# Scaled bias copies behind the relus, the flag's sum an iteration later, new steps and scatter times of the last blocks, and second buffers, in a fused graph network kernel

## The chip, the cores and the metric

The kernel runs on one core of one Trainium2 chip. The metric is the device time of one execution in microseconds (us), lower is better. A ratio is the mean time of one kernel's fast runs over the mean of the other's fast runs of the same rounds, so it is not quite the ratio of the medians that stand beside it.

The span of a profiled execution is about 1.7 us shorter than its time (613.8 us and 615.49 us for the kernel before). Spans and points in time below are those of the trace.

In the profile's lines PE is TensorE, PEld its weight loads, DVE is VectorE, ACT ScalarE and POOL GpSimd; L567 is line 567 of that run's file, so numbers differ by a few between kernels. Of the tiles, z, hps, hT, mu and ma are in PSUM (TensorE's results), y and h are the relus of the two layers, sh the deviations of layer 0, ys the scatter sum of the messages, and uh, uy and uo the stages of a block's update.

## The reference, cut to what matters

There are 128 graphs of 64 nodes with 128 features, and an adjacency matrix for each.

```python
def _layernorm(x, g, b):
    mu = jnp.mean(x, axis=-1, keepdims=True)
    var = jnp.mean(jnp.square(x - mu), axis=-1, keepdims=True)
    return (x - mu) * jax.lax.rsqrt(var + EPS) * g + b

def _mlp(x, w0, b0, g0, be0, w1, b1, g1, be1, w2, b2):
    h = jax.nn.relu(x @ w0 + b0)
    h = _layernorm(h, g0, be0)
    h = jax.nn.relu(h @ w1 + b1)
    h = _layernorm(h, g1, be1)
    return h @ w2 + b2
# ... (f_i, f_j: the features of both ends of each pair of nodes)
pair_feats = jnp.concatenate([f_i, f_j], axis=-1)
messages = _mlp(pair_feats, msg_w0, ...) * coupling_matrix[..., None]
agg = jnp.sum(messages, axis=2)
upd_in = jnp.concatenate([part_feats, agg], axis=-1)
updated = part_feats + _mlp(upd_in, upd_w0, ...)
```

## The kernel before

The kernel packs the existing edges into chunks of 512 slots and runs the message MLP on these chunks only: 160 chunks (NCHK), in 32 groups of five (QC). The 128 graphs form 16 blocks of ten chunks, each with one update MLP. Everything is placed by hand: `at(n, place, f)` puts a step into iteration n, and each iteration runs its places in a fixed order. Each engine's instructions then stand in the order in which they were issued.

```python
L1 = QC + 3                  # layer 1 of chunk n-8 runs in iteration n
for n in range(last + 1):
    run(n, "a")
    run(n, "m")
    if 0 <= n - L1 < NCHK:
        layer1(n - L1)       # z (TensorE), y = relu(z) (ScalarE)
    run(n, "b")
    if n < NCHK:
        layer0(n)            # hps (TensorE), h = relu (ScalarE)
    if 0 <= n - 1 < NCHK:
        stats0(n - 1)        # transposes hT (TensorE), bn_stats (VectorE)
    run(n, "k")
    if 0 <= n - L1 < NCHK:
        stats1(n - L1)
    for k in ("x", "x1", "x2", "e0", "e1", "e"):
        run(n, k)
```

The tile z has one PSUM bank, and so have hT and mu. In the last chunks, layer 1 takes turns between the banks of z and hps. The steps of a block's update are placed by a tuple t of offsets. STEADY serves blocks 0 to 12, and LAST serves the last three blocks. The last block is done in two halves.

```python
STEADY = (1, 2, 3, 3, 4, 7, 8, 6, 8, 9, 12, 13, 11, 14, 15)
# ...
at(n + t[4], "m", layer_out, u, "uh", "m0")    # uh = relu(mu + m0), statistics
at(n + t[7], "a", upd_root0, u)                # um_sd, the standard deviation
at(n + t[7], "a", upd_shift, u)                # usdb
at(n + t[8], "x", lambda u: layer(u, ("uhT", W["u1c"])), u)
at(n + t[9], "m", layer_out, u, "uy", "usdb")  # uy = relu(mu + usdb)
# ...
at(n + t[13], "x", lambda u: layer(u, ("uyT", W["u2c"])), u)
at(n + t[14], "m", finish, u)                  # uo (VectorE), output DMA

def upd_shift(u):
    u.usdb = wide("usdb", u)
    for q in range(u.n):
        nc.scalar.activation(u.usdb[:, q, :], W["bu1b"], AF.Copy, scale=u.sd[:, q:q + 1])
```

A flag at the end tells whether any graph had too many edges for the packed path. Its sum is a small matmul into the one mu bank, and VectorE reads it from there.

```python
at(NCHK - 3, "x", flag_sum)      # FL["b"] = ubank(), one matmul
at(NCHK - 1, "m", flag_out)      # read by VectorE
```

## Time and profile before

| what | value |
|---|---|
| time, median of three runs | 615.79 us (615.77 to 616.52) |
| span of the profiled execution | 613.8 us |
| TensorE busy | 94% of the span |
| first load for z (start of the steady part) | 35.71 us |
| block 12's last layer, mu from u2c (end of the steady part) | 556.27 us |
| end of the last uo | 609.81 us |
| period of a block | 35.11 us |

The table cuts the span in four: the start up to 35.71 us, a steady part of 520.56 us, a tail of 53.54 us and some 4 us of closing output.

The view of busy time by stretches gives, for each stretch, its length, then the busy time of PE, PEld, DVE, ACT and POOL with the number of instructions, then the granted TensorE clock (PEclk, 1.00 is full), the share of the DMA engines and GB/s. In the tail of the kernel before:

```profile
560.00:562.00 2.00, 2.00 (x12) 2.00 (x10) 0.00 (x0) 0.56 (x1) 0.00 (x0) 0.52 0.81 213
562.00:564.00 2.00, 2.00 (x15) 1.83 (x15) 0.72 (x4) 0.82 (x3) 0.00 (x0) 0.62 0.36 82
```

TensorE is fully busy here and runs at half clock for most of it: 2.00 x (1 - 0.52) + 2.00 x (1 - 0.62) = 1.7 us of full-speed work are lost. This stretch follows the wait of 2.1 us for uo. The end of the tail, behind a third long wait of 2.2 us (for uy of block 15, ending at 603.23), is at half clock too:

```profile
606.00:608.00 2.00, 1.49 (x7) 1.19 (x7) 0.60 (x4) 1.02 (x4) 0.14 (x1) 0.50 0.01 4
```

### The profile page before, as it was taken

Reading aid. Unit: us, or ns where it says so; the run is one execution under the profiler, and the core shown is the slowest. Engines: PE = TensorE matmul, PEld = TensorE weight load, DVE = VectorE, ACT = ScalarE, POOL = GpSimd, SP = SyncE. Lnnn points to the kernel's source line nnn. Section 1 sums busy time; section 2 is a strip of 40 time slices with the busy share of each in tenths; the row PEclk is TensorE's granted clock in tenths of the full one; section 3 lists DMA queues with packets and bytes.
Section 4 is the critical chain, followed back from the end, with each engine's and each line's share of the span. In section 5 each row is a group of like instructions: output and inputs, shape, how many; then the busy total and the mean of one; then the engine's idle time right before and its main releaser. Section 6 shows DMA issues by size and latency. Waiting matters only on the chain.

```text
span 613.8 us, 15572 instructions
## 1 busy us (share of the span) xinstructions
PE 579.7 (94%) x5393; PEld 535.0 (87%) x5393; DVE 480.0 (78%) x1947; ACT 397.4 (65%) x845; POOL 296.3 (48%) x837
## 2 busy tenths in 40 slices
PE   5898999999999999999999999999999999998884
PEld 4686889898989999998999989898999999898783
DVE  5657688897979788797978879797978878784685
ACT  5666566776766567766766677676656776653433
POOL 1532455554636565453646555463656545343442
PEclk9989999999999999999999999999999999998996
DMA  4654535544455545644544554345453443531101
GB/s 109 145 126 116 105 88 134 98 123 91 109 140 99 130 90 132 115 99 120 117 122 102 131 102 124 88 112 139 109 134 77 119 116 92 104 87 40 33 9 38
DMA packets 91087, 63.86 MB, mean 104 GB/s; under 512 B 57462, under 2 KB 74876, under 8 KB 91004
## 3 DMA queue, kind: packets, MB, share of 16 engines
q1 hardware_dynamic: 90716, 62.69, 44.5%
q8 instruction: 44, 0.72, 0.5%
q14 instruction: 39, 0.32, 0.2%
q10 hardware_dynamic: 288, 0.13, 0.1%
HBM read 6.82 MB, written 4.19 MB: 18 GB/s over the span
## 4 chain that ended last, share of the span: by engine, by line
PE 82%; ACT 7%; DVE 6%; issue 1%; POOL 1%; DMA 1%; SPq 0%; DVEq 0%; ACTq 0%; POOLq 0%
PE z L566 20%; PE hps L516 12%; PE ys L645 11%; PE hT L525 10%; PE mu L704 8%; PE z L563 7%; PE mu L437 4%; PE ma L690 3%; PE mk L490 3%; ACT usdb L726 2%; ACT y L569 2%; PE ma L423 1%; DVE st L576 1%; ACT abh L446 1%; DVE st L529 1%
## 5 line engine op out<-in xcount | busy, mean ns | idle before, releaser
L529 DVE BATCH_NORM_STATS2 st<-hT 128x6 f32<-128x128 f32 x640 | 142.0, 284 | 67.0 <-PE hT L525 66.1
L566 PEld LDWEIGHTS z<-w1c,h 128*128 128x128 f32 x1248 | 164.6, 192 | 6.6
L566 PE MATMUL z<-w1c,h 128*128 128x128 f32 x1248 | 165.2, 275 | 0.0
L576 DVE BATCH_NORM_STATS2 st<-y 128x6 f32<-128x128 f32 x640 | 137.2, 276 | 4.0 <-ACT y L569 4.0
L569 ACT ACTIVATE y<-z 128x512 f32<-128x512 f32 x156 | 92.7, 594 | 65.9 <-PE z L566 65.3
L247 POOL TENSOR_TENSOR m_d<-st 128x20 f32<-128x20 f32 x62 | 15.7, 254 | 224.3 <-DVE st L529 199.6
L519 ACT ACTIVATE h<-hps,b0c 128x512 f32<-128x512 f32 x160 | 109.2, 682 | 3.3 <-PE hps L516 3.2
L632 POOL TENSOR_TENSOR w<-oh,m_q 128x320 f32<-128x320 f16 x126 | 91.1, 739 | 17.9 <-issue 12.0
L525 PE MATMUL hT<-ident,h 128*128 128x128 f32 x640 | 98.3, 277 | 0.0
L516 PE MATMUL hps<-s,abl 128*128 128x512 f32 (+3 forms) x256 | 92.9, 374 | 0.4 <-ACT h L519 0.4
L525 PEld LDWEIGHTS hT<-ident,h 128*128 128x128 f32 x640 | 77.1, 142 | 9.9 <-DVE st L529 0.3
L563 PE MATMUL z<-b1t,sdT 80*128 80x512 f32 x156 | 76.3, 489 | 6.0 <-ACT y L569 6.0
L516 PE MATMUL hps<-s,abh 128*128 128x512 f32 (+3 forms) x256 | 79.3, 328 | 0.0
L446 ACT CAST abh<-mu 128x512 fp32r<-128x512 f32 x32 | 18.7, 585 | 91.9 <-PE mu L439 91.9
L645 PE MATMUL ys<-y,w 128*64 128x128 f32 x1280 | 77.4, 275 | 0.1
L645 PEld LDWEIGHTS ys<-y,w 128*64 128x64 f32 x1280 | 69.4, 137 | 7.5 <-issue 7.0
L498 DVE TENSOR_TENSOR j<-mk,cmpt 128x320 fp32r<-128x320 f32 x126 | 59.5, 472 | 1.6 <-PE mk L490 1.6
L462 ACT ACTIVATE d<-slot,mid 128x640 f16<-128x640 f16 x64 | 53.3, 833 | 0.0
L516 PEld LDWEIGHTS hps<-s,abl 128*128 128x128 f32 x256 | 50.1, 196 | 1.8 <-ACT i L474 0.9
L516 PEld LDWEIGHTS hps<-s,abh 128*128 128x128 f32 x256 | 50.2, 196 | 0.0
L474 ACT CAST i<-tp 128x640 fp32r<-128x640 f16 x63 | 45.2, 717 | 1.8 <-DVE tp L468 1.8
L453 DVE TENSOR_TENSOR abl<-mu,abh 128x512 fp32r<-128x512 f32 x32 | 22.1, 690 | 27.9 <-ACT abh L446 27.7
(225 smaller groups left out, 991.4 us busy)
## 6 DMA issues: line engine op xcount, KB each, us to landing
s<-i SPq DMA_DIRECT2D x126, 160.0 KB, 2.7
s<-j SPq DMA_DIRECT2D x126, 160.0 KB, 2.6
xn<-in_x_dram SPq DMA_DIRECT2D x15, 256.0 KB, 3.8
out_dram<-uo SPq DMA_DIRECT2D x15, 256.0 KB, 2.4
an<-in_adj_dram SPq DMA_DIRECT2D x16, 128.0 KB, 2.7
oh<-tp SPq DMA_TRANSPOSE x64, 2.7
xn<-in_x_dram SPq DMA_DIRECT2D x2, 128.0 KB
out_dram<-uo SPq DMA_DIRECT2D x2, 128.0 KB
```

The costliest lines, as they stand in the source:

```text
L462: nc.scalar.activation(D[p], slot, AF.Abs, bias=blocks[b]["mid"][:, q:q + 1], scale=-1.0)
L498: nc.vector.tensor_tensor(JR[p][:, c], MK.pop((p, k))[:, 0:HC], cmpt[:, c], op=ALU.is_equal)
L516: nc.tensor.matmul(ps[:, c:c + w], lhsT=ab[:, g % 4, :], rhs=s, start=(k == 0), stop=(k == 1))
L519: nc.scalar.activation(H[n], ps, AF.Relu, bias=b0c)
L525: nc.tensor.transpose(ps[:, t, :], H[n][:, t * P:(t + 1) * P], ident)
L529: nc.vector.bn_stats(ST0[q][:, CH * c + t, :], ps[:, t, :])
L563: nc.tensor.matmul(ps, lhsT=SD[q], rhs=W["b1t"][:, CH * c:CH * c + CH, :], start=True, stop=False, skip_group_check=True)
L566: nc.tensor.matmul(ps[:, t, :], lhsT=h[:, t * P:(t + 1) * P], rhs=W["w1c"], start=False, stop=True, skip_group_check=True)
L569: nc.scalar.activation(Y[n], ps, AF.Relu)
L576: nc.vector.bn_stats(ST1[q][:, CH * c + t, :], Y[n][:, t, :])
L632: (nc.vector if p == NP - 2 else nc.gpsimd).tensor_tensor(WT[p][:, :, g, :], OH[p][:, :, g * N:(g + 1) * N], Q[q][:, k:k + TG].unsqueeze(2 ...
L645: nc.tensor.matmul(YS[b][g * N:(g + 1) * N, k, :], lhsT=w[:, t, g, :], rhs=y, start=(t == 0), stop=(t == TG - 1))
```

## The change

The intent: take the scaled bias copies (usdb) out of the way of the relu y that frees the z bank; shorten the tail by reordering the steps of the last blocks, the scatter weights and the flag; and allow more overlap with second buffers. The core of the diff:

```diff
         def centred(w, g, name):
-            wg = const.tile([P, C], F32, name=name + "_g")
             def product():
+                wg = W[name, "g"] = const.tile([P, C], F32, name="wg", bufs=2)
 # ... (beb likewise, shared in two buffers)
-                                        bufs=2 if name in ("uo", "xo") else 1)
+                                        bufs=2 if name in ("uo", "xo", "m0") else 1)
 # ... steps of blocks 13, 14 and the two halves of 15
-        LAST = ((1, 2, 3, 3, 4, 5, 6, 6, 6, 7, 8, 9, 9, 9, 10),
-                (0, 4, 5, 5, 6, 7, 8, 8, 8, 9, 10, 11, 11, 11, 12),
-                (1, 1, 2, 2, 3, 3, 4, 5, 4, 6, 6, 7, 7, 7, 8),
+        LAST = ((1, 2, 3, 3, 4, 5, 6, 6, 8, 9, 10, 11, 11, 11, 12),
+                (0, 5, 6, 6, 7, 7, 8, 8, 8, 9, 9, 10, 10, 10, 11),
+                (2, 2, 3, 3, 4, 4, 5, 5, 5, 6, 6, 7, 7, 7, 8),
                 (1, 1, 2, 2, 3, 3, 4, 4, 4, 5, 5, 6, 6, 6, 7))
-                    units = [units[0][:3] + (2, 0)]
+                    units = [units[0][:3] + (-5, -4)]
-                units = [(Unit(b, 2, 2, nc.vector, zbank), NCHK + L1 + 1, LAST[3], 1, -3),
-                         (Unit(b, 0, 2, nc.gpsimd, hbank), NCHK + L1, LAST[2], 2, -2)]
+                units = [(Unit(b, 2, 2, nc.vector, zbank), NCHK + L1 + 1, LAST[3], 1, 1),
+                         (Unit(b, 0, 2, nc.gpsimd, hbank), NCHK + L1 - 1, LAST[2], 3, 3)]
-                at(n + t[7], "a", upd_shift, u)
+                at(n + t[7], "x", upd_shift, u)
 # ... (scatter weights, reduce, root_of, turn_root, root_out, root1_of of the
 #      last groups: an iteration earlier or later)
-        at(NCHK - 3, "x", flag_sum)
-        at(NCHK - 1, "m", flag_out)
+        at(NCHK - 2, "x", flag_sum)
+        at(NCHK, "m", flag_out)
 # ...
+            if n == NCHK:
+                stats0(n - 1)
             if 0 <= n - L1 < NCHK:
                 layer1(n - L1)
 # ...
-            if 0 <= n - 1 < NCHK:
+            if 0 <= n - 1 < NCHK - 1:
                 stats0(n - 1)
```

More of the change, by code (lines that the diff above doesn't have):

```diff
@@ L184, in empty @@
                 W[name] = const.tile([P, C], F32, name=name)
-                nc.vector.tensor_tensor(W[name], wg, ps[:, :C], op=ALU.subtract)
+                nc.vector.tensor_tensor(W[name], W.pop((name, "g")), ps[:, :C], op=ALU.subtract)
             return product, empty
@@ L199, in shift @@
         def shift(w, be, bias, name):
-            beb = const.tile([P, P], F32, name=name + "_b")
             def fn(ps):
+                beb = const.tile([P, P], F32, name="beb", bufs=2)
                 nc.scalar.copy(beb, be.to_broadcast([P, P]))
@@ L829, in edge_path @@
             for g in range(2):
-                late = h if q == NQ - 3 else (2 * h + g + 1) // 2
-                at(*((NCHK + L1, "b") if last else (q * QC + QC + L1 + 2 + late, "e1")), weights, p, g)
-            at(NCHK + L1 + 1 if last else q * QC + SC - (q == NQ - 3), "x1", reduce, p)
+                wait = h + 2 if q == NQ - 3 else h + 1 if q == NQ - 2 else 2 + (2 * h + g + 1) // 2
+                at(*((NCHK + L1, "b") if last else (q * QC + QC + L1 + wait, "e1")), weights, p, g)
+            at(NCHK + L1 + 1 if last else q * QC + SC - (q >= NQ - 3), "x1", reduce, p)
         for q in range(NQ):
@@ L837, in edge_path @@
             at(*((n, "e1") if last else (n + 1, "b")), root_of, q)
-            at(n + 1, "b" if last else "x", turn_root, q)
-            at(*((n + 1, "x") if last else (n + 2, "a")), root_out, q)
+            at(*((n + 2, "b") if last else (n + 1, "x")), turn_root, q)
+            at(n + 2, "x" if last else "a", root_out, q)
             at(n + L1 - last, "e1", var1_step, q)
-            at(n + L1 + (0 if last else 2), "a", root1_of, q)
-            at(n + L1 + (0 if last else 2), "m", inverse_of, q)
+            wait = 0 if last else 1 if q == NQ - 2 else 2
+            at(n + L1 + wait, "a", root1_of, q)
+            at(n + L1 + wait, "m", inverse_of, q)
         warm = ubank()
```

## The prediction

> **What bounds the kernel now.** I read the page first: engine shares, then the chain that ended last.
>
> ```profile
> span 613.8 us, 15572 instructions
> PE 579.7 (94%) x5393; PEld 535.0 (87%) x5393; DVE 480.0 (78%) x1947; ACT 397.4 (65%) x845; POOL 296.3 (48%) x837
> PE 82%; ACT 7%; DVE 6%; issue 1%; POOL 1%; DMA 1%; SPq 0%; DVEq 0%; ACTq 0%; POOLq 0%
> ```
>
> TensorE is the bound: 82% of the chain lies on it. The busy table by stretches gives PE 49.1 to 49.6 of every 50 us between 100 and 500 us, but 17.7 of 22 in 558 to 580 and 6.0 of 14 in the last stretch. So a saving counts in two places only: waits of PE inside the steady part, and the tail after about 557 us. Next I asked whom PE's weight loads waited for.
>
> ```profile
> PEld z L563 <- ACT y L569: 9.4, 14, 0.7
> ...
> PEld ma L549 <- DVE sh L544: 3.1, 1, 3.1
> ...
> PEld mu L929 <- DVE uo L740: 2.1, 1, 2.1
> ```
>
> The first is steady: once per block, every 35.1 us. There is a single PSUM bank for z, so a chunk's layer-1 matmul needs the relu (y, ACT) of the chunk before to have read it. The other two are single waits of the tail. One such block, ScalarE's timeline (start, duration, engine, line, operation):
>
> ```profile
> 353.43 0.58 ACT L446 CAST abh<-mu 128x512 fp32r<-128x512 f32 x1 [3.12 <-PE mu L439]
> 353.91 0.30 ACT L257 ACTIVATE um_sd<-um,eps_c 128x4 f32<-128x4 f32 x1
> 354.25 1.28 ACT L726 ACTIVATE usdb<-bu1b,um_sd 128x128 f32<-128x128 f32 x4
> 355.43 0.57 ACT L569 ACTIVATE y<-z 128x512 f32<-128x512 f32 x1
> 355.91 0.67 ACT L519 ACTIVATE h<-hps,b0c 128x512 f32<-128x512 f32 x1
> 356.48 0.72 ACT L474 CAST i<-tp 128x640 fp32r<-128x640 f16 x1
> 357.09 0.83 ACT L462 ACTIVATE d<-slot,mid 128x640 f16<-128x640 f16 x1
> 357.82 0.30 ACT L271 ACTIVATE m_sq<-m_v,eps_c 128x20 f32<-128x20 f32 x1
> 358.02 0.58 ACT L569 ACTIVATE y<-z 128x512 f32<-128x512 f32 x1
> ```
>
> and PE's weight loads beside it:
>
> ```profile
> 356.06 0.19 PEld L563 LDWEIGHTS z<-b1t,sdT 80*128 80x128 f32 x1 [0.69 <-ACT y L569]
> ...
> 358.66 0.19 PEld L563 LDWEIGHTS z<-b1t,sdT 80*128 80x128 f32 x1
> ```
>
> The four scaled bias copies (usdb) stand ahead of y, so y starts 0.7 us late and PE waits 0.69. But see what follows: from 353.91 ScalarE has no gap until the next y ends at 358.60, and PE comes to the next z at 358.66 with no idle time noted. That second z is on the edge already. The trace holds a control: the first block has no update yet, hence no usdb.
>
> ```profile
> 75.88 0.60 ACT L569 ACTIVATE y<-z 128x512 f32<-128x512 f32 x1 [0.73 <-PE z L566]
> ...
> 78.49 0.59 ACT L569 ACTIVATE y<-z 128x512 f32<-128x512 f32 x1
> ```
>
> ```profile
> 79.14 0.19 PEld L563 LDWEIGHTS z<-b1t,sdT 80*128 80x128 f32 x1 [0.49 <-ACT y L569]
> ```
>
> There y waits only for its matmul, and PE stalls at the second z instead.
>
> **What the Trainium skill says.** (1) "TensorE: Matmul & The Clock Gate", section "Architectural detail": the ACT and DVE queues are strictly first in, first out. The trace agrees: y at 355.43 stood behind usdb though z was computed at 354.70. (2) "ScalarE: Activation LUTs", section "What ACT_TABLE_LOAD costs": 186 ns + 0.833 ns per column, about 93 ns for a pointer operand, and neighbours overlap by about 93 ns. For 128 columns that is 386 ns; the trace has a median of 387, and 1.18 us from usdb's start to y's. (3) The first page, section "Part 1: The HAM clock gate": the array falls to half clock after an idle window of about 3.4 us. The stretches agree on the half: after the 2.1 us wait for uo the granted clock reads 0.52 in 560 to 562 and 0.62 in 562 to 564. Yet the 3.1 us wait for sh at 572 to 575 was followed by 1.00, so which stall trips it I can't foretell. (4) "SBUF — State Buffer", section "SBUF: two separate sides": VectorE and GpSimd lock a shared port. The last variance steps on VectorE (m_v, m_s, m_d) took 0.74 us beside GpSimd's multiplies, and 0.18 without: it agrees.
>
> **The change part by part.**
>
> *Bias copies behind the relus (13 steady blocks, usdb at 108 to 530 us).* The order listing shows sd, y, h, usdb, i, d, m_sq, y instead of sd, usdb, y, h, i, d, m_sq, y; nothing is removed. Now y starts when z is ready: by the control 1.31 us after abh (74.57 to 75.88), so at 353.43 + 1.31 = 354.74. It ends near 355.33, and PE, free at 355.37, no longer waits: 0.69 won. But usdb now lies between the two y's. From y to y the control takes 78.49 - 75.88 = 2.61 us; with usdb's 1.18 that is 3.79. The second y starts at 354.74 + 3.79 = 358.53 and ends at 359.11, so PE's second z loads at 359.17, where it loaded at 358.66. PE reaches it at 358.66 - 0.69 = 357.97 and stalls 1.2 us. ScalarE now idles half a microsecond before the first y, and that lands on the path, so each block loses 359.17 - 358.66 = **0.51 us**. PE has no slack later in the block to win it back. 13 x 0.51 = **+6.6 us**.
>
> *Flag's sum an iteration later.* It used the one mu bank right after block 12's last layer and had to wait for uo. Now z of the next iteration goes first. PE is free at 557.27 rather than 559.44. The flag still waits for uo, which now stands behind block 14's bias (m0, 4 operations, 1.12 us, moved ahead of it): uo ends at 560.3, PE arrives at 559.85, so a stall of 0.5 is left. The 40-matmul ys load starts at 560.5 instead of 563.8: -3.3 us, of which about 1.8 is the half clock that I expect not to be tripped here.
>
> *stats0 of the last chunk before layer 1; steps of blocks 13 to 15; scatter times.* The transposes hT of chunks 158 and 159 now stand together, with one bank, so the second waits for VectorE's statistics: about 1.0 us lost (565.1 to 566.1). In return the last layer-0 deviation (sh) comes at 571.1, not 574.9, and hps, u1c and z fill the wait: of 3.1 us about 0.35 is left. Walking on through queues in their listed order, with rows' durations: ys at 571.2; hps, uy, z, u2c, hps, z, hps until 580.5; the second last ys at 580.5 (before: 588.8, but then with the ysum layer ahead of it). VectorE's last variance runs from 582.3 to 583.4 with GpSimd idle (before 587.5 to 590.3, slowed by the port). Its weights are ready at 585.9, the mu layer (1.75 us) ends at 586.3, and the last ys runs 586.4 to 588.8, where it ended at 595.0: -6.2 us in all. After it, the before kernel needs 14.8 us to its last uo (609.8). By the same walk the new order needs 13.4 (block 15's halves no longer go back to front, and its bias is computed early): last uo at 602.2. Tail: 609.8 - 602.2 = **-7.6 us**. The closing 4.0 us of output DMA stay.
>
> *Second m0 buffer, wg and beb shared in two buffers.* Capacity only; each is written again only iterations (2 us and more each) after its last reader: 0.
>
> Sum: 615.8 - 7.6 + 6.6 = **614.8 us**.
>
> **Rivals.** (a) *The steady stall simply goes.* Then 13 x 0.69 = 9.0 us are saved and, with the tail, the time is 615.8 - 9.0 - 7.6 = 599 us, faster by 2.7%. For it: the noted wait does vanish. Against it: ScalarE's gapless run to 358.60 and the control's stall of 0.49. It would need i or d to run elsewhere. (b) *The tail yields little*: the new transpose stall, a half-clock window tripped by it (about 1.7 us each), or the copy chain of block 15's halves on ScalarE takes the saving. With a tail of only -3, 615.8 + 6.6 - 3 = 619.4. For it: every tail wait stands on another engine's queue, and my walk assumes no new surprise. (c) *The steady loss is smaller*, if h or the DMA-fed casts already pad the run: with 0.2 a block, 615.8 + 2.6 - 7.6 = 610.8. I see no padding in the rows.
>
> **Range and chances.** The steady term rests on two measured blocks; I give it +5.5 to +7.5. The tail is a walk of some 45 us by hand; -5 to -9. Taken together, 80% is 611.8 to 617.6. Two per cent is 12.3 us, so faster means under 603.5, which needs rival (a): 5%. Slower means over 628.1, for which both terms must go wrong: 1%.
>
> **What would show it.** Steady: the wait of z on y is still there once a block, now near 1.2 us in place of 0.69, at the second z; the period grows from 35.11 to about 35.6 us. If the period shrinks to 34.4, rival (a) holds and my reading of ScalarE's queue is wrong. Tail: a wait of about 0.5 us for uo at the flag; no half-clock window near 560; a new wait of about 1 us of hT on VectorE; sh's wait below 0.5; from the flag's uo to the last uo about 42 us (before 50.5). If half clock appears inside the tail, rival (b).

## More of the kernel before

The timed executions quoted here were all in the fast state. The one exception is a single execution of one experiment, whose state is unknown, and that is said there.

## The result, and the profile after

The changed kernel took 613.11 us (median of four runs, 611.84 to 613.53) against 615.93 us of the kernel before in the same rounds (four runs, 615.77 to 616.52). The ratio is 0.9949, with a 95% interval of 0.9932 to 0.9966: the same within 2%, and 0.5% shorter.

The head of the page of the changed kernel:

```profile
span 611.1 us, 15571 instructions
PE 574.7 (94%) x5393; PEld 530.1 (87%) x5393; DVE 479.3 (78%) x1947; ACT 397.2 (65%) x845; POOL 294.8 (48%) x837
```

The span fell by 2.7 us, the work is the same, and TensorE is still the bound. The chain of work that ended last can't be used here: in this trace it stops after a single step on VectorE. So I cut both spans in four, as above, by the starts of the same instructions:

| | start | steady part | tail | closing output | span |
|---|---|---|---|---|---|
| before | 35.71 | 520.56 | 53.54 | 4.0 | 613.8 |
| after | 33.56 | 527.32 | 46.36 | 3.9 | 611.1 |
| difference | -2.15 | +6.76 | -7.18 | -0.1 | -2.7 |

The change does two opposite things of about equal size. Whom the weight loads of the changed kernel waited for (total us, times, longest us):

```profile
PEld z L561 <- ACT y L567: 15.1, 14, 1.1
...
PEld hT L523 <- ACT h L517: 1.3, 1, 1.3
...
PEld ma L547 <- DVE sh L542: 0.7, 1, 0.7
PEld mu L928 <- DVE uo L738: 0.6, 1, 0.6
```

The steady wait for y, 9.4 us before, has grown to 15.1 us. The two long waits of the tail (3.1 for sh and 2.1 for uo) have shrunk to 0.7 and 0.6, the third (2.2 for uy) to 0.4, and a new one of 1.3 has come at hT. The view names h for that one, but this h had ended at 570.03, 0.7 us before the load at 570.77. The matmul's own line in TensorE's timeline names VectorE's statistics (st), which ended at 570.65:

```profile
570.80 0.63 PE L523 MATMUL hT<-ident,h 128*128 128x128 f32 x4 [1.08 <-DVE st L527]
```

ScalarE's timeline in one block, the same place as in the prediction (start, duration, engine, line, operation, and in brackets the idle time before it and what ended that):

```profile
354.93 0.59 ACT L444 CAST abh<-mu 128x512 fp32r<-128x512 f32 x1 [3.13 <-PE mu L437]
...
356.24 0.60 ACT L567 ACTIVATE y<-z 128x512 f32<-128x512 f32 x1 [0.53 <-PE z L564]
...
357.30 1.27 ACT L724 ACTIVATE usdb<-bu1b,um_sd 128x128 f32<-128x128 f32 x4
...
360.02 0.58 ACT L567 ACTIVATE y<-z 128x512 f32<-128x512 f32 x1
```

and the weight loads of TensorE that follow those two y:

```profile
356.89 0.19 PEld L561 LDWEIGHTS z<-b1t,sdT 80*128 80x128 f32 x1
...
360.65 0.19 PEld L561 LDWEIGHTS z<-b1t,sdT 80*128 80x128 f32 x1 [1.13 <-ACT y L567]
```

The first y now starts as soon as z is there, with ScalarE idle for 0.53 us before it, and its z no longer waits. But usdb lies between the two y, which are 360.02 - 356.24 = 3.78 us apart, and the second z waits 1.13 us. From abh to that second load it was 358.66 - 353.43 = 5.23 us before and is 360.65 - 354.93 = 5.72 us now: 0.49 us more in this block. From block to block the first kernel's period is 35.11 us and the second's 35.63 us.

In the tail, the stretch by busy time in which the flag's wait for uo ends (at 564.98):

```profile
564.00:566.00 2.00, 1.61 (x24) 1.34 (x24) 2.00 (x10) 1.21 (x3) 1.50 (x4) 1.00 0.05 14
```

The clock stays at 1.00, here and in every stretch of the tail in which TensorE still works.

### The profile page after: what moved, and what is told of

Its sections match the earlier page's. It is cut to its first block, busy times and chain, and to the rows that moved or that the text cites. A ratio compares the mean times of both kernels' runs of the same rounds, so it can differ in the third digit from the quotient of the medians.

```text
span 611.1 us, 15571 instructions
## 1 busy us (share of the span) xinstructions
PE 574.7 (94%) x5393; PEld 530.1 (87%) x5393; DVE 479.3 (78%) x1947; ACT 397.2 (65%) x845; POOL 294.8 (48%) x837
## 5 line engine op out<-in xcount | busy, mean ns | idle before, releaser
L245 POOL TENSOR_TENSOR m_d<-st 128x20 f32<-128x20 f32 x62 | 17.1, 276 | 229.7 <-DVE st L527 206.3
L561 PEld LDWEIGHTS z<-b1t,sdT 80*128 80x128 f32 x156 | 29.4, 189 | 21.9 <-ACT y L567 15.1
```

The costliest lines, as they stand in the source:

```text
L561: nc.tensor.matmul(ps, lhsT=SD[q], rhs=W["b1t"][:, CH * c:CH * c + CH, :], start=True, stop=False, skip_group_check=True)
```

## The experiments

The theory after the result: (1) the steady loss is all due to where usdb stands in ScalarE's queue, (2) the tail's gain is due to the flag and the new steps together, (3) the buffers do nothing, (4) the start is chance. Eleven runs were made, three of them repetitions, all with correct results. This is the cut of their profiled executions:

| kernel | start | steady part | tail | span |
|---|---|---|---|---|
| before | 35.71 | 520.56 | 53.54 | 613.8 |
| after | 33.56 | 527.32 | 46.36 | 611.1 |
| copies_only | 32.56 | 527.09 | 55.42 | 619.5 |
| copies_back | 34.23 | 520.58 | 46.90 | 605.6 |
| copies_early | 32.80 | 512.24 | 46.33 | 595.3 |
| buffers_only | 32.74 | 520.76 | 53.60 | 611.5 |
| early_stats_back | 34.33 | 512.26 | 46.07 | 596.7 |
| early_again | 34.28 | 512.14 | 46.36 | 596.7 |
| flag_only | 34.26 | 520.59 | 51.55 | 610.2 |
| copies_twice | 35.81 | 550.34 | 46.34 | 636.4 |
| steps_only | 33.16 | 520.74 | 50.82 | 608.6 |
| after_again | 34.21 | 527.31 | 46.34 | 611.8 |
| buffers_again | 33.23 | 520.62 | 55.50 | 613.6 |

Steady part and tail move independently to within about half a microsecond, so their effects can be added.

### The copies alone, undone, and moved to an idle place

**copies_only**: the kernel before, with one line of the change.

```diff
-                at(n + t[7], "a", upd_shift, u)
+                at(n + t[7], "x", upd_shift, u)
```

> The kernel before with one edit: the four scaled bias copies are issued after the two relus of the same iteration. My theory (they now lie between the two relus y of which the second frees the z bank): 13 blocks x 0.52 us, so about 622.6 us, wait of z on y 1.13 us a block, period 35.63 us. Rival (the copies were simply in the way): 13 x 0.69 us less, 606.9 us, period 34.4 us. The start can differ by about 2 us between runs (clock).

Measured: 622.27 us (621.18 to 622.84) against 615.45 us (seven runs, 612.94 to 617.36), ratio 1.0126 (1.0081 to 1.0171). The whole interval lies above 1. The steady part is 527.09 us, as in the changed kernel, and in the timeline of the weight loads a typical block has this line:

```profile
181.43 0.19 PEld L563 LDWEIGHTS z<-b1t,sdT 80*128 80x128 f32 x1 [1.11 <-ACT y L569]
```

So this one line makes practically the whole steady loss (+6.5 of +6.8 us). The tail was 1.9 us longer than in the kernel before, which nobody had expected. The view of busy time by stretches has half clock after both of its long waits, for uo and for sh:

```profile
564.00:566.00 2.00, 2.00 (x11) 2.00 (x10) 0.00 (x0) 1.12 (x2) 0.00 (x0) 0.50 0.80 197
578.00:580.00 2.00, 1.73 (x8) 1.63 (x9) 1.07 (x5) 1.15 (x3) 1.84 (x5) 0.50 0.00 0
```

The kernel before had only the first of the two in its profile. This comes back below.

**copies_back**: the changed kernel with that line as it was before.

```diff
-                at(n + t[7], "x", upd_shift, u)
+                at(n + t[7], "a", upd_shift, u)
```

> The changed kernel with only the copies put back ahead of the relus. My theory: the steady loss of 13 x 0.52 = 6.7 us goes, the tail's gain of 7.2 us stays: about 607 to 609 us, period 35.11 us, faster than both kernels. Rival (the copies' move was part of the gain): slower than the changed kernel's 613.1 us.

Measured: 607.13 us (606.19 to 607.44), ratio 0.9872 (0.9827 to 0.9916) to the kernel before. In the timeline of the weight loads, the wait of z is what it was before the change:

```profile
354.59 0.19 PEld L561 LDWEIGHTS z<-b1t,sdT 80*128 80x128 f32 x1 [0.69 <-ACT y L567]
```

The steady part is 520.58 us, and the tail (46.90 us) keeps the gain. So the rest of the change is worth about 1.3%, and the copies behind the relus give most of it back.

**copies_early**: the changed kernel, with the root and the copies of the steady blocks one iteration earlier, at the end of the iteration. The thought: the first line of ScalarE's timeline in the prediction says that it sat idle for 3.12 us before abh. Work put there delays no relu.

```diff
-                at(n + t[7], "a", upd_root0, u)
-                at(n + t[7], "x", upd_shift, u)
+                early = u.b < NB - 3
+                at(n + t[7] - early, "x" if early else "a", upd_root0, u)
+                at(n + t[7] - early, "x", upd_shift, u)
```

> The changed kernel with the deviation and the four copies of the steady blocks issued one iteration earlier, ahead of the cast abh, where ScalarE sits idle for 3.1 us waiting for TensorE. My theory: neither y is delayed, z no longer waits (0 to 0.1 us), period 35.11 - 0.69 = 34.42 us, and with the tail about 615.9 - 9.0 - 7.2 = 599.7 us. If the order on ScalarE is not what stalls z, the wait stays at 0.69 or 1.13 and the time near 607 or 613 us.

Measured: 597.69 us (596.75 to 599.94), ratio 0.9734 (0.9685 to 0.9782), faster. ScalarE's timeline in a block:

```profile
343.13 1.28 ACT L724 ACTIVATE usdb<-bu1b,um_sd 128x128 f32<-128x128 f32 x4
346.04 0.58 ACT L444 CAST abh<-mu 128x512 fp32r<-128x512 f32 x1 [1.62 <-PE mu L437]
347.35 0.60 ACT L567 ACTIVATE y<-z 128x512 f32<-128x512 f32 x1 [0.73 <-PE z L564]
...
349.96 0.59 ACT L567 ACTIVATE y<-z 128x512 f32<-128x512 f32 x1
```

The idle time before abh has shrunk from 3.12 to 1.62 us, and nothing stands between the two y that needn't. They are 349.96 - 347.35 = 2.61 us apart, as in the first block, which the prediction used as its control. Of the 14 waits of z for y only the one of the first block is left (0.5 us), and the steady part is 15.1 us shorter than in the changed kernel: 13 blocks at 1.16 us, the wait that was removed. The same instructions in the same number cost 6.8 us more than before in one place and 8.3 us less in another.

**copies_twice**: the changed kernel with the copies issued twice in the steady blocks (the same values, so the result is right). It was run once, with a profile and without timed rounds, so its state is unknown.

```diff
                 at(n + t[7], "x", upd_shift, u)
+                if u.b < NB - 3:
+                    at(n + t[7], "x", upd_shift, u)
```

> The changed kernel with the four copies of the steady blocks issued twice in the same place. Theory (all that stands on ScalarE between the two relus is on the path): wait 1.13 + 1.18 = 2.31 us a block, period 36.8 us, total 613 + 13 x 1.18 = 628 us within 2 us. Rival (the 1.13 us is a fixed cost of another kind): 613 us.

Measured: 638.09 us. In the waits of the weight loads z is as expected; the time is 10 us above:

```profile
PEld z L561 <- ACT y L567: 30.2, 14, 2.3
```

The start was 2.25 us longer than in the changed kernel's profile, and the steady part 23.0 us longer. Of these, 13 x (2.29 - 1.13) = 15.1 us are the longer waits. The rest, 8 us, lies in five of the blocks. Here is the busy time by stretches of one such block, after its wait that ends at 375.30:

```profile
375.00:377.00 2.00, 1.70 (x10) 1.66 (x10) 2.00 (x11) 1.29 (x3) 0.94 (x5) 0.74 0.65 159
377.00:379.00 2.00, 2.00 (x11) 1.84 (x10) 0.27 (x1) 1.68 (x5) 1.62 (x4) 0.50 0.00 0
```

In the block before it, the same wait ends at 338.52 and the clock reads 1.00 throughout. So a wait of 2.3 us has two prices: itself, and in five blocks of 13 a half-clock stretch that costs 1.6 us more. The mechanism of the theory holds (the wait follows the length of what lies between the two y). The sum that I had expected left this term out.

### The buffers

**buffers_only**: the kernel before with wg and beb shared in two buffers and the second m0 buffer, nothing else of the change.

> The kernel before with the buffers of the change alone (wg and beb shared in two buffers, a second m0). The profile of the changed kernel had its first z 2.1 us earlier than the kernel before. If that was the phase of the clock's half-speed windows at the start: 615.9 us within some 1.5 us, and the period unchanged at 35.11. If the buffers did it: about 613.8 us in every run, first z near 33.6 us.

Measured: 615.75 us (613.22 to 616.3), ratio 1.002 (0.9975 to 1.0064). The steady part and the tail are those of the kernel before within 0.2 us, and so is the period of 35.11 us. The buffers alone do nothing.

### The last statistics

**early_stats_back**: copies_early, with the last chunk's statistics back behind layer 1.

```diff
-            if n == NCHK:
-                stats0(n - 1)
-            if 0 <= n - 1 < NCHK - 1:
+            if 0 <= n - 1 < NCHK:
```

> copies_early with one part of the change undone: the last chunk's transposes and statistics go back behind layer 1 of the same iteration. Tail is counted from the last layer of block 12 to the last output operation (46.3 us in copies_early). My theory: the early place costs TensorE a wait of 1.3 us for VectorE and ScalarE between the two groups of transposes and lets z of chunk 152 start later, whose statistics hold up the deviation sh; undone, sh comes 0.5 to 0.8 us sooner, tail 45.5 to 45.8, total about 597 us. Rival (this part won the 3.1 us wait for sh): tail 48 to 49 us, total about 600 us.

**early_again**: copies_early itself once more, beside it on the same chip.

> copies_early once more, unchanged, beside the other on the same chip: 597.7 us within 1.5 us, steady stretch 512.2 us, tail 46.3 us.

Measured: 598.21 us (five runs, 596.48 to 598.37), ratio 0.9715 (0.9694 to 0.9736), and 597.09 us (six runs, 596.8 to 600.07), ratio 0.9717 (0.9694 to 0.974). The waits of the weight loads of early_stats_back, and then of early_again:

```profile
PEld ma L547 <- DVE sh L542: 1.5, 1, 1.5
...
PEld hT L523 <- DVE st L527: 0.3, 1, 0.3
```

```profile
PEld hT L523 <- ACT h L517: 1.3, 1, 1.3
...
PEld ma L547 <- DVE sh L542: 0.7, 1, 0.7
```

Moving the statistics ahead trades 0.8 us of the wait for sh against 1.0 us of a new wait at hT. The tails are 46.07 and 46.36 us. I had expected a gain of 0.5 to 0.8 us from taking it back; 0.3 us in one trace each, with equal ratios, shows neither gain nor loss.

### The flag and the steps

**flag_only**: the kernel before with the flag's sum an iteration later.

```diff
-        at(NCHK - 3, "x", flag_sum)
+        at(NCHK - 2, "x", flag_sum)
```

The read of the flag couldn't be moved with it. With the read also at its new iteration, as the change has it, a check ahead of any run found a deadlock: with the old steps, block 13's layer asks for the one mu bank before the flag is read from it. So this part of the change needs the new steps.

> The kernel before with the flag's sum alone moved one iteration later (the flag is read out at its old place, for block 13's layer takes the bank next). Theory: TensorE no longer waits 2.1 us for uo and the half clock at 560 us does not come: tail 53.5 - 3.3 to 3.8, so about 50 us, total about 612 us. Rival (later waits take it back): tail 53 us, total 615 us. The start can differ by 2 us, so the tail in the trace decides.

Measured: 611.9 us (611.25 to 613.56), ratio 0.9956 (0.993 to 0.9981). The wait for uo is gone, but the tail is only 2.0 us shorter, where I had expected 3.3 to 3.8. The wait for sh stayed at 3.1 us, and the stretches after it show where the rest went (a line of the weight loads' timeline, then the busy time by stretches):

```profile
569.75 0.14 PEld L549 LDWEIGHTS ma<-ident,sh 128*80 128x80 f32 x1 [3.13 <-DVE sh L544]
```

```profile
570.00:572.00 2.00, 2.00 (x10) 1.90 (x9) 0.98 (x5) 1.04 (x3) 1.42 (x3) 0.50 0.00 0
572.00:574.00 2.00, 2.00 (x15) 1.88 (x14) 0.23 (x2) 0.60 (x1) 0.00 (x0) 0.74 0.00 0
```

The half-clock stretch (1.00 + 0.52 = 1.5 us lost) has only moved from behind the one wait to behind the next.

**steps_only**: the changed kernel with the copies, the flag and the last statistics as before, so only the new steps and scatter times of the last blocks (and the buffers) are left.

> The changed kernel with three of its parts undone: the bias copies are ahead of the relus again, the flag's sum and read are at their old iterations, and the last statistics stand behind layer 1 again. What is left of the change is the new steps and scatter times of blocks 13 to 15 and the buffers. Theory (the tail's gain of 7.2 us is the sum of about 2.0 of the flag's move, about 0 of the statistics and the remainder of about 5 of the new steps): steady part 520.6 us as in the kernel before, tail about 48 to 49 us (before 53.5, changed 46.4), median about 609 to 611. Rival 1 (the flag's move and the steps only pay together, as the flag's read holds the one mu bank in front of block 13's layer and block 14's steps): tail 51 us or more, median 612 to 615. Rival 2 (the steps alone make the whole gain, the flag's stall being absorbed): tail 46.5, median 607.

Measured: 610.62 us (609.58 to 611.86), ratio 0.9919 (0.9894 to 0.9945). The tail is 50.82 us, 2.7 us shorter than before. That is nearer to the first rival (51 us or more) than to my theory (48 to 49 us). The wait for sh is down to 1.3 us, but the flag now waits longer than in the kernel before, since block 14's bias stands in front of uo on VectorE, and half clock follows (the weight load of the flag, and the stretch after it):

```profile
558.00 0.08 PEld L928 LDWEIGHTS mu<-mean_m,f 2*1 2x1 f32 x2 [3.13 <-DVE uo L738]
```

```profile
558.00:560.00 2.00, 2.00 (x10) 1.87 (x11) 0.00 (x0) 0.00 (x0) 1.27 (x1) 0.50 0.51 147
```

The third wait, for uy, is gone with the half clock behind it, which all five profiles with the old steps have.

So, by these traces, the flag alone is worth 2.0 us, the steps alone 2.7, and both together 6.6 (copies_back, whose copies stand as in these two, against the kernel before; its early statistics are worth 0.3 us at most). The sum of the parts lacks 1.9 us. Each part alone leaves one of the two long waits, with a half-clock stretch of 1.5 to 1.7 us behind it; with both, there is no wait over 1.6 us left in this part of the tail and no half clock. (The tail of the changed kernel is another 0.5 us shorter than that of copies_back: that is the copies of the last blocks.)

But this count rests on which execution of the kernel before was profiled. Its profile has half clock behind one of the two waits. Against the tail of 55.50 us that the same order has when both are followed by it (buffers_again, below), the flag is worth 4.0 us, the steps 4.7 and both 8.6: they add up. The timed ratios add up too, within their noise: 0.44% and 0.81% for the parts, 1.28% for both. Shown is that with one wait gone, the half clock stood behind the other in both traces. That the parts as such don't add up isn't shown.

### The start

**after_again** and **buffers_again**: the changed kernel and buffers_only once more, in five rounds. What was open: the traced parts, steady and tail, differ by -0.4 us, yet the times differ by 2.8 us, and the start of the two profiles differs by 2.15 us.

> The changed kernel itself once more, in five rounds beside the kernel before. The traces give the steady part and the tail together a difference of -0.4 us (+6.76 and -7.18), and the start of the two profiled executions another -2.15. Theory (the start's difference is chance: which half-clock window the first 36 us catch differs from run to run, and each kernel shows all of it): the median of the changed kernel over six runs comes nearer to the kernel before, difference -0.4 to -1.5 us, with single runs between 611.5 and 616. Rival (the changed kernel really starts earlier, as its own four runs of 611.84 to 613.53 suggest): the median stays 612.5 to 613.5 and the difference -2.3 to -3 us, and hardly a run lies above 614.

> The kernel before with the shared buffers alone (wg, beb and m0 in two buffers) once more, in five rounds: the only part of the change that touches the first 36 us. Theory (chance): its median within 0.5 us of the kernel before, its single runs between 612 and 617 as those of the kernel before. Rival (the shared buffers of the preparation make the start 2 us shorter): median 612.8 to 613.5, as the one profiled run of it, and few runs above 615.

Measured: after_again 612.19 us (six runs, 611.99 to 613.58), ratio 0.9954 (0.993 to 0.9978), and buffers_again 615.76 us (six runs, 614.85 to 616.21), ratio 1.0012 (0.9988 to 1.0037), beside the kernel before at 615.19 us (eleven runs, 612.53 to 617.27).

The number of the rival came true: the medians differ by 3.0 us, where my theory said 0.4 to 1.5. The changed kernel's ten runs all lie within 611.84 and 613.58, and those of the kernel before scatter over 5 us, mostly above. But the start, the rival's cause, isn't what sets the kernels apart: it was 34.21 us in the new profile of the changed kernel and 33.23 in that of buffers_again, which is the slower one. The tail is. In buffers_again it took 55.50 us instead of 53.60, with two half-clock stretches, one behind the flag's wait and one behind the wait for sh (3.13 us, ending at 572.48). The view of busy time by stretches of buffers_again:

```profile
558.00:560.00 2.00, 2.00 (x11) 2.00 (x10) 0.00 (x0) 0.97 (x2) 0.00 (x0) 0.51 0.76 196
...
574.00:576.00 2.00, 2.00 (x11) 2.00 (x10) 0.18 (x1) 0.65 (x3) 0.23 (x1) 0.50 0.00 0
```

So of the old tail's waits for uo and sh, in some executions one, in others both are followed by half clock. The profile of the kernel before was of the first kind.

What the start goes by can be read from the length of TensorE's matmuls. In the seven profiles with a start of 34.2 us or more, the 128-column products for mu at 6 us take 0.42 us (in the other six 0.27), and matmuls are that slow until about 20 to 22 us. In the two with 35.7 us and more they are slow again from 31.6 us on. Both kinds occur with and without the change. The granted clock reads 1.00 all through this slow stretch, so at the head of these traces it can't be trusted.

A check by sums, as an estimate: the mean start of the 13 profiles is 33.9 us. With it, 4.0 us of closing output and 1.7 us from span to time, the changed kernel should take 33.9 + 527.3 + 46.4 + 5.7 = 613.3 us (measured 613.11 and 612.19), copies_only 622.1 (622.27), flag_only 611.7 (611.9), steps_only 611.2 (610.62). The kernel before should take 613.7 us with the tail of its profile and 615.7 us with that of buffers_again; its medians were 615.19 to 615.93. So most of its executions should be of the second kind. The spans and mean clocks of its 36 executions timed beside the experiments point the same way: 11 have a clock of 0.977 to 0.980 and 612.6 to 614.8 us, like the profile of buffers_again (0.980, 613.6), and six have 0.983 or 0.984 and 610.5 to 611.4 us, like that of buffers_only (0.984, 611.5; one of the two waits followed by half clock). The rest can't be told apart, as only profiled executions have a trace.

## Why the prediction was right

The time (614.8 predicted, 613.11 and 612.19 measured) held. By its own steps:

- **Bias copies, +6.6 us: right in cause and size.** The traces give +6.76 us (after) and +6.5 us (copies_only alone). The wait went to the second z (1.13 us for the predicted 1.2), and the period to 35.63 us for the predicted 35.6. The two y are 3.78 us apart for 3.79.
- **Rival (a), 599 us: rejected for this change, right as a number.** The prediction said that it "would need i or d to run elsewhere". That was too narrow: copies_early leaves i and d in place and moves usdb into an idle stretch of ScalarE that the prediction's own rows show (3.12 us before abh). It took 597.69 us.
- **The tail, -7.6 us: right in size, -7.18 in the trace pair.** The wait for uo at the flag is 0.63 us (predicted 0.5), ys starts at once after it, there is no half clock, and from the flag's uo to the last uo it takes 607.24 - 564.98 = 42.3 us (predicted about 42). From the end of the last ys to the last uo it is 607.24 - 593.83 = 13.4 us, as predicted (14.1 in copies_back, where the copies of the last blocks stand ahead of the relus), and VectorE's last variance steps take 0.16 to 0.19 us each with GpSimd idle (three had taken 0.74; two of these stood beside GpSimd's additions for xo, not its multiplies, a small misreading). But the split into parts was not right. The flag was given -3.3 us, of which 1.8 for the half clock. Alone it gives -2.0 against the trace that the prediction read, where another wait then takes the half clock, -4.0 against the tail of buffers_again, and 2.7 us by the timed ratio (1.2 to 4.3). The step that failed is the one that treats these 1.8 us as the flag's own: which wait they stand behind differs between executions. That the sum fits the traced pair within 0.4 us is in part luck for the same reason.
- **The new wait at hT: right in size and cause.** It is 1.3 us at the weight load and 1.08 at the matmul, for about 1.0. The prediction put it down to VectorE's statistics and the single hT bank, and the matmul's line names these statistics. The view of the weight loads names h, and in copies_back m_sq, both on ScalarE; but both had ended over 0.5 us before the load, and the matmul waits for the statistics there too (1.07 us). The wait for sh came out at 0.67 us where 0.35 was predicted. Both together are why the early statistics bring nothing.
- **Buffers, 0: right.** Ratios 1.002 and 1.0012.
- **What was not in the sum.** The prediction took the profile of the kernel before as its typical execution. It had a long start (35.71 us) and a short tail (53.54 us), and the two roughly cancel in the total of 615.8. Against the tail of 55.50 us that the same order also has, the change saves 9.1 us rather than 7.2. The measured difference of 2.8 us instead of the predicted 1.0 is of this size. That it comes from there is an estimate, as the section on the start says.

The best version is copies_early, 2.7% faster than the kernel before (and its repetition 2.8%).

## What to carry to other kernels

An instruction moved out of the way of one relu stands in the way of the next one on a strictly ordered queue: before moving it, look for the place where that engine idles and nothing waits on it, and check both neighbours' deadlines. A wait that is no longer reported at its old place isn't gone until the period has become shorter. Where a stall can also halve the clock, one trace doesn't price it: the half clock can stand behind this stall, the next one, or both, so what removing one stall gains depends on the execution that it is compared with. Look at more than one execution's trace, and at the timed runs. And where a view names whom an instruction waited for, check when that one ended: if it was long done, look for another.

## What the Trainium skill lacked or had wrong

- "TensorE: Matmul & The Clock Gate", section "Part 1: The HAM clock gate", gives half clock after an idle window of about 3.4 us, and puts the ramp at under 1% of a typical span. Here shorter waits were enough: 2.1 us in the kernel before (0.52 and 0.62 in the four microseconds after it) and 2.3 us in copies_twice, in five blocks of 13. A wait of 3.1 us was followed by half clock in flag_only, copies_only, steps_only and buffers_again, and wasn't in the kernel before and buffers_only. The page calls the window free-running, which fits that the same wait has it in one execution and not in another, but it gives no lengths or odds for waits shorter than the window. A stretch cost 1.5 us (flag_only) to 1.9 us (between the tails of buffers_only and buffers_again). That is under 1% of 615 us, as the page says, but as much as most parts of this change.
- No page that I read has this: with a single-bank tile in a steady cycle, moving 1.2 us of other work from ahead of one release to behind it delays the next release. A wait of 0.69 us became one of 1.13 us, and the period grew by 0.5 us.
